# Two-layer sequence model on one core: a second unit's queries in other PSUM banks, a key head moved behind the first transposes, a norm's inverse root moved to another engine, and three output projections moved from places 101 and 111 to 73 and 81

## The chip, the cores and the metric

The kernel runs on one core of a Trainium2 chip. The metric is the device time of one execution in microseconds, of which three runs are given. The engines are named as the profile names them: PE multiplies matrices (PEld is its loading of weights), DVE is the vector engine, ACT the scalar engine, POOL the GpSimd engine, and SP issues most of the transfers. PSUM is the memory that PE writes its results to, in banks of 128 partitions by 512 numbers; the other engines read them there.

## The reference

2048 tokens (2 sequences of 1024) of 256 numbers pass two layers. Each layer is attention and then a feed-forward part, each with a residual sum and a norm behind it (x = layernorm(x + part(x))):

- layer 0: softmax attention with rotary positions (32 query heads, 8 key heads, causal), then a gated feed-forward part with 8-bit weights;
- layer 1: a gated delta rule with 16 heads of 128 by 128 state, then a feed-forward part whose weights are only signs.

The delta rule is where the change lies. Per head, q, k and v are projections of x, each passed through a causal convolution over 4 tokens and a silu; alpha and beta are sigmoids of two more projections; and then, token by token,

```
err = S k - v
S   = alpha * S - beta * err k^T
o   = S q
```

The rows o are normalised over 128 numbers per head, scaled by a sigmoid gate g = sigmoid(x Wg), and projected with Wo back to 256 numbers. Everything is float32.

## The kernel before, in words

**Stages.** Layer 0's attention comes first (two passes over the scores, L1267 and L1336), then its feed-forward part (up to about 800 us), then the delta rule (about 800 us to 1950 us), with the early parts of each stage laid into the stage before it, and layer 1's feed-forward part last. Products whose precision matters are made of three matmuls with high and low parts (`mm3`, L962 to L964).

**The delta rule's tiling.** The 2048 tokens are cut into 4 halves of 512, and the 16 heads into 8 pairs. A *unit* is one pair of heads in one half: unit i is half i // 8 and pair i % 8, so there are 32 units. Units 7, 15, 23 and 31 are the last ones of their halves. Inside a unit the tokens go through in 4 chunks of 128, the state M handed on from chunk to chunk (`recur`): transposed v minus the state's part (`pr`, L673 and L677), the copy `prs` on ACT, a product with the inverted triangle (`pw`, L688), the copy `wc` on ACT, the state's product (`pm`, L700) and the output's (`po`, L715 and L716), and the new state M on DVE (L705 or L707).

**The order.** Each unit has 120 *places*, 30 per chunk. Everything beside the recurrence is written as generators that yield the place at which they want to go on; `Places` runs them by that number, and this sets the written order of the program. `InLine` chains all of PE's matmuls in exactly this order from unit 0 on (`te.strict`). On the other engines a scheduler orders the instructions at build time; each engine's queue is then run in order.

In unit i, beside its own recurrence, the places hold work for later units: the next unit's v and q projections (`others`, places 1 and 31, through `pair`), its gate projection (61), its scores `pkq` (`scores`, L508, places 71 and 81), each followed by two products on POOL (`decayed`, L519 and L521) that scale k and q by decays `dg`; the keys of unit i + 4 (`keys`, place 91; the scans L325 on DVE); and for every other unit a solver on DVE (`blocks`, L384 and L390) and a set of small matmuls (`levels`, L420, then L423 on DVE, then L431).

Unit i's own rows are brought to an end in unit i + 1 by `finish`: a norm per head (inverse root on POOL through `rsqrt`, then L599 and the normalising instructions of DVE, ACT and POOL, L606 and L609), at places 41 and 51 the transposes `pt` (L615), then ACT (L618), the gate's product on DVE (L619), a rounded copy `yh` on POOL (L623) and the rest `yl` on POOL (L911); and at two more places the projection `pf` with Wo, 12 matmuls each for two chunks. DVE adds `pf` to the tokens `xtok` (L636). For the last unit of a half the tokens are then complete: a layernorm on DVE (L942, L943, L925 to L932, L946) and a store follow.

```
AT_FINISH, AT_FINISH_LAST, AT_HALF = (41, 51, 101, 111), (31, 41, 71, 76), ((22, 30, 46), (8, 13, 20))
```

The first two of each four are the places of `pt`, the other two those of `pf`.

**PSUM in the delta rule.** Tag `p` has 2 banks (projections and their convolutions), `m` has 2 (triangles, scores, keys' transposes), `c` has 2 (the recurrence), `t` has 1 (`pt` and `pf`), `l` has 1 (the levels).

**A projection's way.** `project` writes one head's product into a bank. `conv` reads it there on ACT and with two instructions on DVE (L275, the taps), `conv_out` reads it a last time on ACT (`far`, L289), and POOL adds `far` (L292). The bank is free after L289.

**The start.** Before the strict order begins, `rest_of_first` scales unit 0's k and q, projects unit 1's v and q and unit 4's k, in that order, all into the two `p` banks. At the same time layer 0's feed-forward part ends: its last block of 256 tokens is normalised (`layernorm`, with the inverse root on POOL, L934 to L937) and stored. `anchor["norm"]` is the last instruction of that norm (L946); the solver of unit 2 is ordered behind it.

Of the kernel before, what the change touches and what calls it, by code (L numbers as in the profile page):

```python
# [22 lines left out]
NT = B * T // P  # L23
# [8 lines left out]
HP = 2  # L32
NS = H // HP
# [44 lines left out]
AHEAD = 4  # L78
# [6 lines left out]
AT_ROWS, AT_QUERIES, AT_KC, AT_GATE, AT_GATE_ROWS, AT_SCORES = 1, 31, (42, 52), 61, 70.5, (71, 81)  # L85
AT_OUT = 9.5
# [2 lines left out]
AT_LEVELS = 43, 53, 73, 83, 103, 113, 132, 142  # L89
AT_FFN = 24  # L90
AT_FINISH, AT_FINISH_LAST, AT_HALF = (41, 51, 101, 111), (31, 41, 71, 76), ((22, 30, 46), (8, 13, 20))

FFN0, FFN1, FFN1_LAST, FFN1_TAIL = 7.6, 22.0, 27.0, 40.0

# [50 lines left out]
def delta_rule(  # L145
# [13 lines left out]
    nc = tc.nc  # L159
# [8 lines left out]
    ps_p = open_pool(left, "ps_p", "left", 2, PSUM)  # L168
    ps_m = open_pool(left, "ps_m", "left", 2, PSUM)
# [15 lines left out]
    def bank(pool, tag, name):  # L185
        return pool.tile([P, HT], F32, name=name, tag=tag)
# [49 lines left out]

        return divmod(i, NS)

    def project(m, i, h):
        hi, s = place(i)  # L240
        if h == 0 and ("w" + m) not in st[i]:
            st[i]["w" + m] = weights(m, s)
        wh, wl = st[i]["w" + m]
        xh, xl = halves[hi]["xh"], halves[hi]["xl"]
        pp = bank(ps_p, "p", "pp")
        hs = slice(h * P, (h + 1) * P)
        for k in range(2):
            mm3(pp, wh[:, k, hs], wl[:, k, hs], xh[:, k, :], xl[:, k, :], k == 0, k == 1)
        return pp
# [10 lines left out]
    def conv(m, i, h, pp):  # L260

        hi, s = place(i)
        n, hd = "qkv".index(m), s * HP + h
        acc = half_tile(early if m == "k" else conv_pool, m, 10 if m == "k" else 4)
        st[i][m, h] = acc

        with tc.high_priority():
            nc.scalar.activation(  # L268
                acc, pp, AF.Identity, bias=cb[:, n, hd : hd + 1], scale=cw[:, n, hd, KS - 1 : KS]
            )  # L270
            if hi % 2 == 0:
                nc.scalar.copy(halos[:, n, hd, :], pp[:, HT - KS + 1 :])  # L272

            for d in range(1, KS - 1):
                made = nc.vector.scalar_tensor_tensor(  # L275
                    acc[:, d:], pp[:, 0 : HT - d], cw[:, n, hd, KS - 1 - d : KS - d], acc[:, d:], ALU.mult, ALU.add
                )
                if m == "k" and d == 1 and solved:
                    after(made, solved[-1])
        return made  # L280
# [18 lines left out]
    def keys(i, t0):  # L299

        hi, s = place(i)
        col = halves[hi]["col"]
        pps = [project("k", i, h) for h in range(HP)]
        if i < last:
            st[i + 1]["wk"] = weights("k", place(i + 1)[1])
        for h in range(HP):
            taps = conv("k", i, h, pps[h])
        yield t0 + AT_OUT
        for h in range(HP):
            conv_out("k", i, h, pps[h])  # L310
        yield t0 + AT_DECAY - AT_KEYS
        lt = early.tile([P, U, P], F32, name="lt", tag="lt", bufs=4)
        st[i]["lt"] = lt
        nc.gpsimd.memset(lt[:, :, 0:1], 0.0)
        for h in range(HP):
            hd = s * HP + h
            dec = decay(hi, hd, 0, "da")
            d1 = early.tile([P, HC, P], F32, name="d1", tag="raw", bufs=RAW)
            nc.gpsimd.affine_select(
                d1, col[:, :, hd].unsqueeze(2).to_broadcast([P, HC, P]),  # L320
                pattern=[[0, HC], [1, P]], compare_op=ALU.is_equal, fill=0.0, base=0, channel_multiplier=-1,
            )
            e = half_tile(early, "at", 10)
            after(
                nc.vector.tensor_tensor_scan(e, dec, d1.rearrange("p c t -> p (c t)"), 0.0, ALU.mult, ALU.add), taps  # L325
            )
            st[i]["at", h] = e

            em = early.tile([P, HC], F32, name="em", tag="em", bufs=10)
            nc.gpsimd.tensor_scalar(em, q4(e)[:, :, P - 1], -SCALE, None, ALU.mult)  # L330
            st[i]["em", h] = em
        for h in range(HP):
            yield t0 + AT_TRIANGLE[h] - AT_KEYS
            e, k = st[i]["at", h], st[i]["k", h]
            pkk = bank(ps_m, "m", "pkk")
            for c in range(HC):
                t = slice(c * P, (c + 1) * P)
                te.link(nc.tensor.matmul(pkk[:, t], lhsT=k[:, t], rhs=k[:, t], start=True, stop=True))
            nc.vector.scalar_tensor_tensor(
                lt[:, h * HC : (h + 1) * HC, 1:P], q4(pkk)[:, :, 1:P], SCALE, q4(e)[:, :, 0 : P - 1],  # L340
                ALU.mult, ALU.mult,
            )
        yield t0 + AT_TRIANGLE[2] - AT_KEYS
        n = i % 2
        if n == 0:
            st[i]["d1"] = dram.tile([Q, 2 * U, BL, BL], F32, name="d1_", tag="d1_")
        else:
            st[i]["d1"] = st[i - 1]["d1"]
        for q in range(Q):
            r = slice(q * BL, (q + 1) * BL)  # L350
            nc.sync.dma_start(
                out=st[i]["d1"][q, n * U : (n + 1) * U].rearrange("u j t -> j u t"), in_=lt[r, :, r]
            )
# [124 lines left out]
                    te.link(nc.tensor.matmul(p4[A, u, :], lhsT=n3[Z, u, :], rhs=lt[Z, u, Z], start=True, stop=True))  # L478
            nc.scalar.copy(st[i + n]["lt"][A, :, Z], p4[A])

    def pair(m, i):

        pps = [project(m, i, h) for h in range(HP)]
        for h in range(HP):
            conv(m, i, h, pps[h])
        if i < last:
            yield AT_OUT
        for h in range(HP):
            conv_out(m, i, h, pps[h])
# [68 lines left out]
    def rest_of_first():  # L558
        decays(0)
        for which in "kq":  # L560
            for h in range(HP):
                decayed(0, h, which)
        te.strict, te.last = True, ended[0]
        for m in "vq":
            drain(pair(m, 1))
        ks = keys(AHEAD, AT_KEYS)
        next(ks)
        lines.add(ks, next(ks), 0)

    def gate_of_first():  # L570
        gate(0)
        yield GAP
        gate_rows(0)
# [70 lines left out]
    def recur(i):  # L644
# [8 lines left out]
        def moments(c):  # L653
            for h in range(HP):
                st6 = pools["late"].tile([P, 6], F32, name="ost", tag="ost")
                with tc.high_priority() if i == last and c == HC - 1 else nullcontext():
                    nc.vector.bn_stats(st6, o[:, c, h, :])
                    nc.vector.bn_aggr(m[:, c * HP + h, 0:2], st6)
            part = HC // 2 if i == last else HC
            if c % part == part - 1:  # L660
                chunks = range(c + 1 - part, c + 1)
                at = i * UNIT + 3 * GAP * (c + 1) + 3
                lines.add(finish(
                    i, o, m[:, chunks[0] * HP : (c + 1) * HP, :], chunks,
                    AT_HALF[c // part] if i == last else AT_FINISH_LAST if i == last - 1 else AT_FINISH,
                ), at, at if i == last else (i + 1) * UNIT)

        for c in range(HC):
# [166 lines left out]
    def drain(g):  # L835
        for _ in g:
            pass

    for i in range(-AHEAD, last + 1):
# [19 lines left out]
        elif 0 <= i < last:  # L859
            lines.add(others(i + 1), t + AT_ROWS, t)  # L860
        if i == 0:
            lines.add(gate_of_first(), t + AT_QUERIES)
        if i >= 0:
            lines.add(recur(i), t, chain=True)
# [27 lines left out]
def tile_two_layers(ctx: ExitStack, tc: tile.TileContext, a, out):  # L892
# [46 lines left out]
    def layernorm(pool, x, t0, n, tag="ln", eng=None):  # L939
        m = pool.tile([P, n, 11], F32, name=tag, tag=tag)  # L940
        for i in range(n):
            nc.vector.bn_stats(m[:, i, 5:11], x[:, t0 + i, :])  # L942
            nc.vector.bn_aggr(m[:, i, 0:2], m[:, i, 5:11])  # L943
        rsqrt(m[:, :, 2], m[:, :, 1], m[:, :, 3], m[:, :, 4], eng=eng)
        for i in range(n):
            made = nc.vector.tensor_scalar(  # L946
                x[:, t0 + i, :], x[:, t0 + i, :], m[:, i, 0:1], m[:, i, 2:3], ALU.subtract, ALU.mult
            )
        return made
# [16 lines left out]
    def after(later, earlier):  # L966

        tc.add_manual_dep(
            later.ins, earlier.ins.name,
            mybir.DependencyInfo(mybir.DependencyClass.NoSync, mybir.DependencyReason.DATA), reason="order",  # L970
        )
# [507 lines left out]
    def open_ffn(group):  # L1479
# [20 lines left out]
        def block(n):  # L1500
# [45 lines left out]
            with tc.high_priority() if n == NT - 2 else nullcontext():  # L1546
                for i in range(2):
                    y = new("fy", [P, E], 2)
                    nc.vector.tensor_mul(y, po[i], s_down)
                    nc.vector.tensor_add(x[:, n + i, :], y, x[:, n + i, :])  # L1550
                anchor["norm"] = layernorm(pool, x, n, 2, eng=nc.gpsimd)
                store_tokens(xs, n, x[:, n : n + 2, :])
            yield 0.2

# [127 lines left out]
```

## Time and profile before

| what | value |
|---|---|
| median of 3 runs | 2062.5 us (2060.35 to 2066.07) |
| the profiled execution's own time | 2059.24 us |
| its span | 2057.5 us |
| PE busy | 1894.6 us (92%) |
| DVE busy | 1469.6 us (71%) |
| ACT busy | 1271.6 us (62%) |
| POOL busy | 1078.6 us (52%) |
| mean granted PE clock | 0.977 |

How to read it: the span is what the profile covers; 1.74 us of the execution lie outside it. Busy shares are means over the whole span, so they hide single stretches. The rows of the window view give, for a stretch, each engine's busy time and the mean clock that PE was granted (1.00 is full speed). A row of the view of waits says which instruction of an engine stood idle for what, in total microseconds, times, and the longest. A row of the timeline gives start, duration, engine, line and operands; `x4` at its end means four instructions taken together, and what stands in brackets is the idle time before it and what ended it.

### The profile page before, as it was taken

What the parts mean: (1) busy time and instruction counts of PE and PEld (TensorE: products, weight loads), DVE (VectorE), ACT (ScalarE), POOL (GpSimd) and SP (SyncE); (2) the same over time, 40 slices, a digit from 0 to 9 for tenths busy, and PEclk for the clock granted to TensorE, in tenths of its full rate; (3) what the DMA queues carried; (4) which work ended last, traced back from release to release, by engine and by line L of the source; (5) the groups of instructions that cost most, each with busy time, mean ns of one, the idle gap of its engine ahead of it and who ended that gap; (6) DMA issues with size and microseconds to landing.
All of it is one profiled execution on the core that took longest, in us unless ns stands there. A gap on an engine that the chain in (4) does not pass through costs nothing. (4 is left out here: it accounts for less than half of the span.)

```text
span 2057.5 us, 49231 instructions
## 1 busy us (share of the span) xinstructions
PE 1894.6 (92%) x18657; PEld 1494.6 (73%) x18657; DVE 1469.6 (71%) x3469; ACT 1271.6 (62%) x2739; POOL 1078.6 (52%) x1739
## 2 busy tenths in 40 slices
PE   5898989999998998999999999998999999999886
PEld 3455555555555786889888888887988888888775
DVE  5756666877756986586778778678677778865565
ACT  1365556576664466667776776766677676676433
POOL 4353332431124565566776576666567666665452
PEclk9999999999999998999999999999999999999997
DMA  5563443441132432343444434344344434442010
GB/s 169 177 190 126 146 134 127 147 132 65 52 76 62 119 89 90 103 136 104 130 110 121 130 111 130 106 124 119 115 113 118 127 114 132 119 124 81 22 41 21
DMA packets 312998, 229.17 MB, mean 111 GB/s; under 512 B 139640, under 2 KB 278904, under 8 KB 312760
## 3 DMA queue, kind: packets, MB, share of 16 engines
q1 hardware_dynamic: 299640, 210.73, 35.1%
q10 hardware_dynamic: 9760, 10.83, 1.6%
q0 software_dynamic: 3360, 4.46, 0.9%
q8 instruction: 147, 2.41, 0.5%
q14 instruction: 91, 0.75, 0.1%
HBM read 171.18 MB, written 51.87 MB: 108 GB/s over the span
## 5 line engine op out<-in xcount | busy, mean ns | idle before, releaser
L1276 DVE TENSOR_REDUCE mx<-ps 128x4 f32<-128x1024 f32 (+1 forms) x320 | 344.1, 1111 | 129.3 <-PE ps L1267 86.8
L1340 ACT ACTIVATE es<-ps 128x512 f32<-128x512 f32 (+1 forms) x608 | 314.3, 578 | 128.7 <-PE ps L1336 117.1
L1336 PE MATMUL ps<-qT,kT 128*128 128x512 f32 (+3 forms) x768 | 220.7, 371 | 17.8 <-ACT es L1340 16.5
L1267 PE MATMUL ps<-kT,qT 128*128 128x512 f32 x576 | 198.7, 419 | 26.9 <-DVE mx L1276 17.6
L1336 PEld LDWEIGHTS ps<-qT,kT 128*128 128x128 f32 x768 | 130.9, 190 | 104.2 <-ACT es L1340 57.0
L1267 PEld LDWEIGHTS ps<-kT,qT 128*128 128x128 f32 x576 | 101.2, 190 | 86.8 <-DVE mx L1276 47.7
L289 ACT ACTIVATE far<-pp,cw 128x509 f32<-128x509 f32 x192 | 133.4, 700 | 46.3 <-DVE k L275 18.8
L1357 PE MATMUL av<-es,vaug 128*32 128x512 f32 (+3 forms) x1536 | 157.1, 495 | 0.7 <-POOL es L1343 0.7
L1343 POOL TENSOR_SCALAR_AFFINE_SELECT es<-es 128x512 f32<-128x512 f32 x128 | 80.5, 639 | 145.8 <-ACT es L1340 143.5
L911 POOL TENSOR_TENSOR wfl<-wf,wfh 128x256 fp32r<-128x256 f32 x80 | 58.7, 735 | 186.1 <-ACT wfh L1000 160.4
L275 DVE SCALAR_TENSOR_TENSOR q<-pp,cw,q 128x511 f32<-128x511 f32 (+1 forms) x128 | 93.2, 742 | 47.1 <-ACT halos L272 23.2
L275 DVE SCALAR_TENSOR_TENSOR k<-pp,cw,k 128x511 f32<-128x511 f32 (+1 forms) x128 | 92.2, 743 | 45.8 <-ACT k L268 25.1
L292 POOL TENSOR_TENSOR q<-q,far 128x509 f32<-128x509 f32 x64 | 69.4, 1087 | 95.3 <-ACT far L289 95.2
L275 DVE SCALAR_TENSOR_TENSOR v<-pp,cw,v 128x511 f32<-128x511 f32 (+1 forms) x128 | 92.2, 739 | 33.3 <-ACT v L268 18.2
L292 POOL TENSOR_TENSOR k<-k,far 128x509 f32<-128x509 f32 x64 | 77.8, 1217 | 51.2 <-ACT far L289 50.6
L519 POOL TENSOR_TENSOR k<-k,dg 128x508 f32<-128x508 f32 x64 | 82.2, 1284 | 33.7 <-PE pkq L508 29.4
L716 PE MATMUL po<-wc,at 128*128 128x128 f32 x512 | 97.3, 277 | 0.0
L680 ACT COPY prs<-pr 128x256 f32<-128x256 f32 x128 | 48.8, 382 | 76.5 <-PE pr L677 68.3
L1000 ACT CAST wfh<-wf 128x256 fp32r<-128x256 f32 x80 | 32.4, 405 | 102.5 <-DMA wf<-in_w1k 35.0
L325 DVE TENSOR_TENSOR_SCAN at<-da,d 128x512 f32<-128x512 f32 x64 | 90.4, 1453 | 0.0
L700 PE MATMUL pm<-wc,kc 128*128 128x128 f32 x448 | 77.7, 296 | 11.4 <-ACT wc L691 11.3
L715 PE MATMUL po<-M,q 128*128 128x128 f32 x448 | 87.8, 278 | 0.0
(325 smaller groups left out, 5907.8 us busy)
## 6 DMA issues: line engine op xcount, KB each, us to landing
wk<-w1k SPq DMA_DIRECT2D x64, 256.0 KB
da<-dec SPq DMA_DIRECT2D x64, 256.0 KB
wv<-w1v SPq DMA_DIRECT2D x64, 256.0 KB
wq<-w1q SPq DMA_DIRECT2D x64, 256.0 KB
dg<-dec SPq DMA_DIRECT2D x64, 256.0 KB
wg<-w1g SPq DMA_DIRECT2D x64, 256.0 KB
wo<-w1o SPq DMA_DIRECT2D x64, 256.0 KB
ad<-avs ACTq DMA_DIRECT2D x32, 256.0 KB
```

What stands on the lines that cost most here:

```text
L275: made = nc.vector.scalar_tensor_tensor(acc[:, d:], pp[:, 0 : HT - d], cw[:, n, hd, KS - 1 - d : KS - d], acc[:, d:], ALU.mult, ALU.add)
L289: made = nc.scalar.activation(far[:, w], pp[:, w], AF.Copy, scale=cw[:, n, hd, 0:1])
L292: nc.gpsimd.tensor_add(acc[:, KS - 1 :], acc[:, KS - 1 :], far[:, w])
L325: nc.vector.tensor_tensor_scan(e, dec, d1.rearrange("p c t -> p (c t)"), 0.0, ALU.mult, ALU.add), taps
L519: nc.gpsimd.tensor_mul(q4(k)[:, :, 1:P], q4(k)[:, :, 1:P], q4(gs)[:, :, 0 : P - 1])
L715: te.link(nc.tensor.matmul(po[:, r], lhsT=st[i]["q", h][:, t], rhs=M[:, r], start=True, stop=False))
L716: te.link(nc.tensor.matmul(po[:, r], lhsT=st[i]["at", h][:, t], rhs=wc[:, r], start=(M is None), stop=True))
L1267: anchor["mm"] = te.link(nc.tensor.matmul(ps[:, j - j0, :].rearrange("p (g k) -> p g k", k=P), lhsT=q_, rhs=kT[:, :, j * P : (j + 1) * P], ...
L1276: nc.vector.tensor_reduce(mx[:, it, j0 // 2, :], ps[:, 0:n, :].rearrange("p j (g k) -> p g j k", k=P), AX.XY, ALU.max)
L1336: te.link(nc.tensor.matmul(ps[:, g - g0, :], lhsT=kT[:, g, jb * P : (jb + 1) * P], rhs=qT[:, i0 : i0 + w], start=True, stop=True,))
L1340: exps.append(nc.scalar.activation(es[:, g0 : g0 + n, 0:w], ps, AF.Exp, scale=D ** -0.5))
L1357: mm = te.link(nc.tensor.matmul(av[ROW * g : ROW * (g + 1), i0 - ih * 512 : 512], lhsT=vaugs[b][:, jb, kv, :], rhs=es[:, g, 0:w], start=(j ...
```

## The change

1. `rest_of_first` projects unit 1's queries into the two `m` banks, while its values stay in the `p` banks. Unit 4's first key head is projected there too; the second key head and all that follows it goes into a stream of its own, `first_keys`, whose next place is after the first chunk has begun, so that the two first `pr` transposes of unit 0 stand ahead of it on PE. One of the taps of unit 1's queries is ordered behind `anchor["norm"]`.
2. The last block of layer 0's feed-forward part takes its norm's inverse root on DVE (three times L930 to L932) instead of POOL (three times L934 to L937).
3. Units 7, 15 and 23 (the last of a half, but for the very last) have their two `pf` groups at places 73 and 81 instead of 101 and 111, behind the scores of the next unit's heads.

```diff
+AT_FINISH_ROWS = 41, 51, 73, 81
...
-    def project(m, i, h):
+    def project(m, i, h, psum=None):
...
-        pp = bank(ps_p, "p", "pp")
+        pp = bank(*(psum or (ps_p, "p")), "pp")
...
+                if m == "q" and i == 1 and d == 1:
+                    after(made, anchor["norm"])
...
-        pps = [project("k", i, h) for h in range(HP)]
+        pps = [st[i].pop("first")] if "first" in st[i] else [project("k", i, 0)]
+        pps.append(project("k", i, 1))
...
-    def pair(m, i):
+    def pair(m, i, psum=None):
...
-        pps = [project(m, i, h) for h in range(HP)]
+        pps = [project(m, i, h, psum) for h in range(HP)]
...
-        for m in "vq":
-            drain(pair(m, 1))
+
+        for m, psum in (("v", (ps_p, "p")), ("q", (ps_m, "m"))):
+            drain(pair(m, 1, psum))
+        st[AHEAD]["first"] = project("k", AHEAD, 0)
+
+    def first_keys():
+
         ks = keys(AHEAD, AT_KEYS)
         next(ks)
-        lines.add(ks, next(ks), 0)
+        yield AT_ROWS + AT_OUT
+        yield next(ks)
+        yield from ks
...
-                    AT_HALF[c // part] if i == last else AT_FINISH_LAST if i == last - 1 else AT_FINISH,
+                    AT_HALF[c // part] if i == last else AT_FINISH_LAST if i == last - 1
+                    else AT_FINISH_ROWS if s == NS - 1 else AT_FINISH,
...
         if i == 0:
+            lines.add(first_keys(), t + AT_ROWS, t)
             lines.add(gate_of_first(), t + AT_QUERIES)
...
-                anchor["norm"] = layernorm(pool, x, n, 2, eng=nc.gpsimd)
+                anchor["norm"] = layernorm(pool, x, n, 2, eng=nc.gpsimd if n < NT - 2 else None)
```

## The prediction

> **What bounds the kernel now.** I read the page first, for which engine is the bound; then the stretches around the four places that the change touches, for clock and gaps; then PE's waits there; then POOL's timeline at the new place of the projections.
>
> ```profile
> PE 1894.6 (92%) x18657; PEld 1494.6 (73%) x18657; DVE 1469.6 (71%) x3469; ACT 1271.6 (62%) x2739; POOL 1078.6 (52%) x1739
> ```
>
> PE is busy for 92% of the span, so a microsecond taken from its idle time or from its half-speed time is a microsecond of the whole, unless the next wait takes it. The places touched are the start of the delta rule (seam 0, 800 us) and the ends of the first three halves (seams 1, 2 and 3: 1112, 1402 and 1702 us). The view by windows there (PE's busy time first, DVE's third, the granted clock after POOL):
>
> ```profile
> 800.00:820.00 20.00, 13.24 (x43) 8.99 (x42) 15.28 (x42) 11.09 (x24) 8.33 (x18) 0.76 0.41 131
> 820.00:840.00 20.00, 18.11 (x101) 15.85 (x102) 10.22 (x33) 8.76 (x24) 10.86 (x11) 0.77 0.64 185
> 1112.00:1146.00 34.00, 29.89 (x446) 26.66 (x445) 33.04 (x111) 21.00 (x46) 23.30 (x35) 1.00 0.42 121
> 1402.00:1428.00 26.00, 24.13 (x160) 21.16 (x159) 24.38 (x75) 15.44 (x37) 15.58 (x17) 1.00 0.46 133
> 1428.00:1444.00 16.00, 8.31 (x160) 7.03 (x159) 10.58 (x40) 7.19 (x16) 9.16 (x19) 0.68 0.34 107
> 1702.00:1730.00 28.00, 26.10 (x263) 22.96 (x263) 26.93 (x94) 16.09 (x33) 20.23 (x31) 1.00 0.47 132
> ```
>
> Seam 0 loses both ways: 6.8 us of gaps in its first window, and a clock of 0.76. At seams 1 to 3 DVE is nearly full (33.0 of 34 us), and PE loses a few microseconds after it. What PE waits for, seam by seam (total, times, longest):
>
> ```profile
> PE pp L962 <- ACT far L289: 5.9, 3, 2.1
> ```
>
> ```profile
> PE px L431 <- DVE n L423: 2.3, 1, 2.3
> PE pm L700 <- ACT wc L691: 1.4, 1, 1.4
> ```
>
> ```profile
> PE pt L615 <- POOL o L609: 7.7, 2, 7.1
> ```
>
> ```profile
> PE p L460 <- issue: 1.6, 1, 1.6
> PE pm L700 <- ACT wc L691: 1.4, 1, 1.4
> ```
>
> So there is 5.9 us to win at seam 0, and at most 3.7, 7.7 and 3.0 us at the others, if the earlier projections relieve DVE.
>
> **Part 1, seam 0: queries in the `m` banks, second key head later, inverse root on DVE.** The three waits for `far` (5.9 us) are for `p` banks. Queries no longer need them, key head 0 comes long after `far` of the values, and key head 1 moves behind the `pr` transposes. These three gaps go. What is late next: chunk 1 needs the state M from DVE (L705 at 824.0), which stands behind the two scans of unit 4's keys (819.83 to 823.9), and the change leaves scans ahead of it; by DVE's order M comes near 819.4, 4.6 us earlier. Then the gate's projection waits for `far` of key head 0, and chunk 1's `wc` copy on ACT stands behind the silu of the keys, which wait for POOL's adds; laid end to end the second `pm` comes at 828 to 829 instead of 831.08, a gain of 2 to 3 us. The inverse root: 12 POOL instructions between 806.63 and 810.87 go, 9 DVE instructions of about 0.15 us (1.35 us) come; the norm's end (813.0), the tokens' store and the `dg` loads queued behind it on SP come some 2 us sooner, and POOL's products, which now wait 2.61 us for `dg`, with them. No one on PE waits for these before chunk 1. Clock: rows here run at half speed from 812.1 to 829.2; fewer gaps may free it, but the waits that remain are of the size that halves it (below). Ends: −5.9 us (all gaps won) and 0 (the chain through M, keys and `wc` takes all). I take −1.5, by the `pm` row, less some for the 1.35 us on DVE and the new waits.
>
> **Part 2, seams 1 to 3: projections at 73 and 81.** The 24 matmuls of a seam cost the same wherever they stand (0.118 us apart, 1.43 us a group). What counts is what they wait for. The first group now stands directly behind `pkq` of head 0, and its sixth matmul reads `yl` of head 1 (L911). POOL's order is the same in both kernels, and there `yl` of head 1 stands *behind* the two products of head 0's decays (L519, L521), the first of which waits for just that `pkq`. Seam 3's timelines, POOL and then PE:
>
> ```profile
> 1703.73 0.61 POOL L623 CAST yh<-y 128x512 fp32r<-128x512 f32 x1 [0.90 <-DVE y L619]
> 1704.53 1.27 POOL L519 TENSOR_TENSOR k<-k,dg 128x508 f32<-128x508 f32 x1 [0.19 <-PE pkq L508]
> 1705.75 1.28 POOL L521 TENSOR_TENSOR q<-q,dg 128x512 f32<-128x512 f32 x1
> 1706.98 1.31 POOL L911 TENSOR_TENSOR yl<-y,yh 128x512 fp32r<-128x512 f32 x1
> ```
>
> ```profile
> 1703.39 1.06 PE L508 MATMUL pkq<-q,k 128*128 128x128 f32 x8
> 1704.29 0.61 PE L700 MATMUL pm<-wc,kc 128*128 128x128 f32 x4
> ```
>
> `pkq` ends at 1704.29 and `yl` at 1708.29: 4.0 us, of which five matmuls cover 0.6. So PE stands still for 3.4 us at each of three seams. Seams 1 and 2 have the same rows (`pkq` ends 1113.49 and 1405.55, `yl` ends 1117.48 and 1409.55). Queued behind the waiting matmul on PE: `pm`, `po`, the second `pkq`, and with them the new M, DVE's scores and POOL's second pair of products. This is certain as far as the orders are.
>
> The stall also costs clock. At 1743.98 PE idles for 1.64 us, and then 512-column matmuls come 0.43 us apart instead of 0.23 until 1750.8:
>
> ```profile
> 1747.40:1750.80 3.40, 3.40 (x10) 2.63 (x9) 0.44 (x1) 2.31 (x6) 0.00 (x0) 0.51 0.00 0
> 1750.80:1754.20 3.40, 3.40 (x34) 3.14 (x34) 2.65 (x6) 1.63 (x3) 1.06 (x2) 1.00 0.37 125
> ```
>
> 3.4 us at half speed lose 1.7 us of work; a 3.4 us stall may hit one or two such stretches, 1.6 to 3.0 us; I take 2.1. [...]
>
> A third term: in the last chunk the old group stood between `pw` and `po` while ACT made `wc`; without it PE waits for `wc`, about 0.7 us (the 0.46 and 1.4 us rows of `pm` from both sides). Each seam so begins at 3.4 + 2.1 + 0.7 = +6.2 us. What comes back, as DVE has its norm work (L636 to L946, some 9 us) earlier:
>
> - Seam 1: the 2.3 us before L431, because the four L946 no longer stand around L423: +3.9. The 1.4 us row could come back too: +2.5; nothing back: +6.2.
> - Seam 2: the normalise of unit 16 (L609) moves ahead of the queries' taps, and most of the norm stands in front of the scans; its last `pt` would end near 1436 instead of 1438.2, −2.2, and the half-speed stretch behind it (to 1443.4, 2.7 us lost) may shrink: −4.9. If DVE's key taps, late by the stall, hold the normalise: +1. I take −1.5.
> - Seam 3: 1.6 of the 3.0 us is "issue" before L460 (the levels), which the change does not touch; 1.4 comes back: +4.8, between +3 and +6.2.
>
> SP: one `dg` load, two `wk` loads move behind the solver's stores and the `wo` loads; `wk` is fetched a whole unit (36 us) ahead, and POOL reaches the second `dg` only behind `yl`: nothing, and at most the 2.61 us that the `dg` row at 818 shows. The second group waits for DVE to have added the first (same `t` bank); `pm`, `po` and `pkq` of 2.5 us lie between, against 0.68 for L636.
>
> **Sum.** −1.5 + 3.9 − 1.5 + 4.8 = +5.7 us on the profiled execution's 2059.24 (span 2057.5 and 1.74 around it), so 2064.9; that execution lies 3.3 us below the median of 2062.5, so 2068.2 beside it. What a measurement can tell from no change is about 0.3%, 6.2 us; the sum lies at that border.
>
> **Rivals.**
>
> 1. *The gaps are won, and clock with them* (faster). Place: seam 0 and seam 2. For it: 5.9 us of waits for banks plainly removed and 0.76 clock (17 us of half speed, some 6 to 8 us of work lost); the 7.1 us wait and its 2.7 us. Against it: the M and `wc` chain, and the stall. Price: −8 at seam 0, −4.9 at seam 2, +2.5 and +3 at the others: −7.4, 2055. It decides once seam 0's clock is back at full speed before 820.
> 2. *DVE becomes the bound behind the stall* (slower still). DVE is 33 of 34 us busy at seam 1; it idles through most of 3.4 us while PE waits, and the keys' taps and scans come late at all three seams. Price: nothing back at any seam, seam 0 zero: 3 × 6.2 = +18.6 at worst, with half of that +9 to +14: 2075.
> 3. *Stall and relief cancel*: the clock is not halved (−6.3 from the sum): 2062, within 0.3%.
> 4. *The stall doesn't occur* as POOL is early: excluded by its order, where L519 waits for `pkq`.
>
> **Numbers.** Forecast (the sum) 0.55, its own range 2062 to 2073, about evenly on both sides of the 0.3% border; rival 1: 0.19; rival 2: 0.17; rival 3: 0.09. Slower: 0.17 + 0.30 = 0.47; within: 0.25 + 0.08 = 0.33; faster: 0.20. The range from 2053 to 2077 leaves out the tails of rivals 1 and 2.
>
> **What would show it.** Waits `pf <- POOL yl` of about 3.4 us, three times, in the chain behind `pkq`, and clock under 1.00 near 1116, 1408 and 1708 would show the stall; the row `pp L962 <- ACT far` gone or near 2 us at 800, and M's copy near 819, seam 0; `px <- DVE n` gone at 1143, and `pt <- POOL o` under 3 us at 1430, the relief. It is wrong if no `yl` wait appears, or if seam 0 alone gives over 6 us.

## The result: 0.55% slower, within the range

The changed kernel takes 2069.69 us (median of 7 runs, 2065.99 to 2080.55), the kernel before, run again beside it, 2060.35 us (7 runs in all, 2055.25 to 2066.07). The ratio is 1.0055, with a 95% interval of 1.0035 to 1.0075: some 7 to 15 us lost. The forecast was 2068.2 us with a slight lean to slower, 1.5 us from the measured time. That it came so near is in part luck: it was the first median of the kernel before, 2062.5 us, plus 5.7 us, and that kernel came out 2.1 us lower when it was run again. What the change itself costs is 11 us by the ratio, about twice the 5.7 us of the sum.

The profiled execution of the changed kernel has a span of 2067.2 us, 9.7 us more than that of before (its own time is 2068.99 us, 9.75 us more). The page's first row shows that PE did the same work, and that DVE did the nine instructions more:

```profile
PE 1895.5 (92%) x18657; PEld 1495.1 (72%) x18657; DVE 1478.8 (72%) x3478; ACT 1270.6 (61%) x2739; POOL 1074.0 (52%) x1727
```

**One ruler for all kernels.** Line numbers and places shift from kernel to kernel, and so does the time at which the delta rule begins: the first value projection starts at 799.9 us in the kernel before, 799.6 in the changed one, and between 801.4 and 810.1 in the experiments, though no kernel alters anything ahead of it except what is named here. A span alone therefore can't carry a difference of a few microseconds. What can is a stretch with the same work in it. I use the starts of the `wc` copy of the first chunk of a unit, read from ACT's timeline: from unit 7 to unit 10 for seam 1, 15 to 18 for seam 2, 23 to 26 for seam 3. The view by windows of the kernel before over these three stretches (stretch, its length, then PE busy with its count; the clock stands after POOL):

```profile
1057.30:1171.04 113.74, 106.70 (x1536) 95.50 (x1537) 86.14 (x249) 76.50 (x165) 73.76 (x122) 1.00 0.44 127
1351.58:1469.96 118.38, 107.81 (x1525) 96.14 (x1526) 84.00 (x233) 78.46 (x184) 71.95 (x116) 0.96 0.42 123
1648.17:1762.37 114.20, 108.52 (x1536) 96.70 (x1537) 85.76 (x249) 76.17 (x165) 74.47 (x121) 0.99 0.42 125
```

and of the changed kernel over the same three:

```profile
1057.33:1175.69 118.36, 106.97 (x1536) 95.28 (x1537) 88.33 (x249) 76.72 (x166) 73.29 (x122) 1.00 0.42 123
1355.98:1472.66 116.68, 106.94 (x1525) 95.55 (x1526) 85.05 (x233) 77.56 (x185) 72.28 (x116) 0.99 0.44 126
1650.25:1770.67 120.42, 110.20 (x1536) 98.31 (x1537) 89.31 (x249) 76.89 (x165) 73.71 (x121) 0.97 0.40 117
```

The counts of PE agree row by row, so length minus busy is idle time, and the two larger differences in busy time at the same count go with the clock of the rows: 1.7 us more at seam 3, with 0.97 against 0.99, and 0.9 us less at seam 2, with 0.99 against 0.96. Seam 1: +4.6 us, nearly all idle (7.0 to 11.4). Seam 2: −1.7 (idle 10.6 to 9.7, busy −0.9). Seam 3: +6.2 (idle 5.7 to 10.2, busy +1.7). Together +9.1 of the 9.75 us; the start gives −0.4, and the rest of the span moves by +1.0. Each of these lengths comes from one profile. Stretches that no edit touches (units 2 to 7, 10 to 15 and 18 to 23, measured in the same way) differ by 0.9, 1.7 and 1.6 us among the twelve profiles of this document, so a difference under some 1.5 us in one stretch says little by itself. At the start the two windows shown before now read:

```profile
800.00:820.00 20.00, 14.13 (x54) 10.55 (x52) 18.67 (x50) 9.74 (x22) 6.54 (x5) 0.76 0.59 192
820.00:840.00 20.00, 16.71 (x94) 14.38 (x94) 8.58 (x37) 10.14 (x26) 10.96 (x13) 0.78 0.47 124
```

PE does more in the first and less in the second; the clock is as low as it was (0.76 and 0.78, before 0.76 and 0.77).

**The stall is there.** PE's waits at seam 3 in the changed kernel (total, times, longest):

```profile
PE pf L977 <- POOL yl L924: 3.3, 1, 3.3
PE pm L712 <- ACT wc L703: 1.6, 1, 1.6
PE pr L689 <- DVE M L719: 1.5, 1, 1.5
PE px L435 <- issue: 1.1, 1, 1.1
```

and the timelines there, POOL's first and then PE's (L523 and L525 are the decay products, L924 is `yl`, L512 the scores, L977 the matmul on `yl`):

```profile
1705.41 0.61 POOL L634 CAST yh<-y 128x512 fp32r<-128x512 f32 x1 [0.90 <-DVE y L630]
1706.21 1.27 POOL L523 TENSOR_TENSOR k<-k,dg 128x508 f32<-128x508 f32 x1 [0.20 <-PE pkq L512]
1707.45 1.26 POOL L525 TENSOR_TENSOR q<-q,dg 128x512 f32<-128x512 f32 x1
1708.67 1.26 POOL L924 TENSOR_TENSOR yl<-y,yh 128x512 fp32r<-128x512 f32 x1
```

```profile
1706.44 0.28 PE L976 MATMUL pf<-wo,yh 128*128 128x256 f32 x1
1709.98 0.58 PE L977 MATMUL pf<-wo,yl 128*128 128x256 f32 x1 [3.27 <-POOL yl L924]
```

`yh` is ready at 1706.02; POOL then does two products that PE does not wait for here, and only afterwards the `yl` that PE waits for. The same 3.3 us appear at seams 1 and 2: 9.8 us in three waits.

### The profile page after: what moved, and what is told of

It is laid out like the page before. It is cut to its first block, busy times and chain, and to the rows that moved or that the text cites. A ratio compares the mean times of both kernels' runs of the same rounds, so it can differ in the third digit from the quotient of the medians.

```text
span 2067.2 us, 49232 instructions
## 1 busy us (share of the span) xinstructions
PE 1895.5 (92%) x18657; PEld 1495.1 (72%) x18657; DVE 1478.8 (72%) x3478; ACT 1270.6 (61%) x2739; POOL 1074.0 (52%) x1727
## 5 line engine op out<-in xcount | busy, mean ns | idle before, releaser
L924 POOL TENSOR_TENSOR wfl<-wf,wfh 128x256 fp32r<-128x256 f32 x80 | 58.5, 734 | 185.0 <-ACT wfh L1013 153.6
L276 DVE SCALAR_TENSOR_TENSOR q<-pp,cw,q 128x510 f32<-128x510 f32 (+1 forms) x128 | 92.9, 743 | 46.1 <-ACT q L269 24.0
L523 POOL TENSOR_TENSOR k<-k,dg 128x508 f32<-128x508 f32 x64 | 81.7, 1276 | 56.7 <-PE pkq L512 47.0
L689 PE MATMUL pr<-M,k 128*128 128x128 f32 x448 | 83.4, 282 | 7.5 <-DVE M L719 3.9
L700 PEld LDWEIGHTS pw<-prs,lt 128*128 128x128 f32 x512 | 76.8, 191 | 18.3 <-ACT prs L692 7.6
```

The costliest lines, as they stand in the source:

```text
L276: made = nc.vector.scalar_tensor_tensor(acc[:, d:], pp[:, 0 : HT - d], cw[:, n, hd, KS - 1 - d : KS - d], acc[:, d:], ALU.mult, ALU.add)
L523: nc.gpsimd.tensor_mul(q4(k)[:, :, 1:P], q4(k)[:, :, 1:P], q4(gs)[:, :, 0 : P - 1])
L689: te.link(nc.tensor.matmul(pr[:, r], lhsT=st[i]["k", h][:, t], rhs=M[:, r], start=False, stop=True))
```

## The experiments

The lengths of the stretches, in microseconds, all from ACT's timelines in one profiled execution each; *start* is from the first value projection to unit 2's first `wc`. The ratio is that of the timed runs to the kernel before, with its 95% interval. The kernel before was run again beside each set: its median was 2060.35 us beside the changed kernel, 2063.7 beside e1 to e4, 2064.3 beside e5 to e8 and 2064.6 beside e9 and e10. So times of different sets are compared here by their ratios.

| kernel | start | seam 1 | seam 2 | seam 3 | ratio |
|---|---|---|---|---|---|
| before | 84.4 | 113.7 | 118.4 | 114.2 | |
| changed | 84.0 | 118.4 | 116.7 | 120.4 | 1.0055 (1.0035 to 1.0075) |
| e1: places 73 and 81 alone | 84.1 | 122.2 | 117.8 | 121.4 | 1.0085 (1.0057 to 1.0113) |
| e2: start alone | 83.9 | 111.0 | 118.0 | 111.0 | 0.9971 (0.9958 to 0.9985) |
| e3: changed, `yl` first | 82.9 | 116.8 | 112.5 | 117.0 | 1.0007 (0.9992 to 1.0023) |
| e4: changed, places 83 and 93 | 83.9 | 120.4 | 112.7 | 113.7 | 1.0002 (0.9986 to 1.0017) |
| e5: start, unit 15 at 83 and 93 | 83.5 | 110.6 | 112.9 | 112.2 | 0.9946 (0.9926 to 0.9966) |
| e6: as e3, norms left out | 83.3 | 113.6 | 110.9 | 111.7 | 0.9949 (0.9932 to 0.9967) |
| e7: as e2, norms left out | 83.8 | 110.8 | 108.7 | 109.9 | 0.9901 (0.9871 to 0.9931) |
| e8: as e2, root on POOL | 85.1 | 110.9 | 118.1 | 111.4 | 0.9999 (0.9985 to 1.0013) |
| e9: as e3, norms behind taps and M | 84.9 | 121.8 | 118.6 | 120.7 | 1.0071 (1.0053 to 1.0089) |
| e10: start, unit 15, `yl` first | 84.7 | 110.9 | 115.8 | 111.9 | 0.9969 (0.9953 to 0.9984) |

### The two halves of the change (e1 and e2)

e1 adds only the new places to the kernel before:

```diff
+AT_FINISH_ROWS = 41, 51, 73, 81
...
+                    else AT_FINISH_ROWS if s == NS - 1 else AT_FINISH,
```

> The kernel before with the places 73 and 81 alone. Theory (the stall of the first projection group on yl, which stands behind the scores' products on POOL, costs the time): three waits of pf on yl of 3.3 us; seam 1 about +5, seam 2 about -2, seam 3 about +6.5 us; whole 8 to 11 us over before. Rival (the start of the delta rule costs the time): not over 3 us.

e2 is the changed kernel without them:

```diff
-                    else AT_FINISH_ROWS if s == NS - 1 else AT_FINISH,
+                    else AT_FINISH,
```

> The change without the places 73 and 81: queries in the scores' banks, second key head later, inverse root on DVE. Theory: no wait on yl, start worth -3 to +1 us, whole 2055 to 2063. Rival (the start costs the time): 6 us or more over before.

Measured: the places alone cost 0.85% (17.5 us, more than the 8 to 11 expected), the start alone gains 0.29% (6 us). The product of the two ratios, 1.0056, is that of the whole change. So the loss is the places', and the rival that the start costs the time is out. The three waits on `yl` are there, 3.3 us each, as expected. The seam stretches of e1 differ from the kernel before by +8.4, −0.6 and +7.2 us, against +5, −2 and +6.5 expected; at seam 1, where the miss is largest, PE also waits 2.2 us for `far` and 1.5 us for M.

The gain of e2 is as expected in size, but it is not where the edit is. Its start is 0.5 us shorter, which is within the scatter; seams 1 and 3 are 2.7 and 3.2 us shorter, where e2 edits nothing. At seam 1, the scheduler, which orders the program as a whole, has put L423's counterpart ahead of more of the norm, and the wait for it falls from 2.3 us to the 0.8 of this row:

```profile
PE px L435 <- DVE n L427: 0.8, 1, 0.8
```

At seam 3, DVE's order is the same as before; what is gone is the 1.6 us gap marked "issue", of which 0.4 is left, and the half-clock stretch that followed it (the clock of the stretch is 1.00 against 0.99 before). All kernels here with the queries in the `m` banks, the norm and the old places at seam 3 (e2, e5, e8 and e10) have 111.0 to 112.2 us there, and the single profile of the kernel before has 114.2; why the gap is shorter in them, I can't say.

### The stall (e3 and e4)

e3 orders the two products of head 0 behind `yl` of head 1 at the three seams:

```diff
+            made = nc.gpsimd.tensor_mul(q4(k)[:, :, 1:P], q4(k)[:, :, 1:P], q4(gs)[:, :, 0 : P - 1])
+            if i > 1 and i % NS == 1 and h == 0:
+                after(made, anchor["yl"])
...
+            made = nc.gpsimd.tensor_mul(q, q, gs)
+            if i > 1 and i % NS == 1 and h == 0:
+                after(made, anchor["yl"])
...
+                anchor["yl"] = sub_low(nc.gpsimd if i < last else nc.vector, yl, y, yh)
```

> The change, with head 0's two decay products (POOL) of units 9, 17 and 25 ordered behind yl of head 1. Theory: the waits on yl fall from 3.3 to under 1.0 us each, no half-speed stretch follows them, and the whole falls by 7 to 15 us against the changed kernel, to 2054 to 2062. Rival (DVE is the bound there, the stall is only where the wait shows): the wait goes and waits on M, wc or far take its place; within 3 us of the changed kernel.

e4 leaves POOL alone and moves the projections on:

```diff
-AT_FINISH_ROWS = 41, 51, 73, 81
+AT_FINISH_ROWS = 41, 51, 83, 93
```

> The change, with places 83 and 93 instead of 73 and 81: the first group stands behind the second head's scores, the second behind the keys' projections. Theory: 2.3 us of PE's work now cover part of the 4.0 us until yl, so waits of about 1.2 us each, too short for half speed; 6 to 12 us under the changed kernel. Rival (DVE is the bound): within 3 us of it.

In e3 the three waits on `yl` sum to 1.8 us, the longest 0.7, no half-clock stretch is left in the three seams (all three rows have a clock of 1.00), and the kernel takes 2066.2 us, some 10 us less than the changed one by the two ratios:

```profile
1066.52:1183.35 116.83, 107.30 (x1536) 95.40 (x1537) 86.65 (x249) 76.70 (x165) 73.47 (x122) 1.00 0.43 124
1363.73:1476.23 112.50, 105.86 (x1525) 93.87 (x1526) 82.01 (x233) 77.89 (x184) 71.80 (x116) 1.00 0.45 129
1654.37:1771.32 116.95, 107.34 (x1536) 95.41 (x1537) 86.97 (x249) 77.08 (x166) 74.23 (x121) 1.00 0.44 122
```

The time of 2066.2 us itself lies above the 2054 to 2062 that was expected, because the kernel before ran 3.4 us slower in this set; the fall of some 10 us is inside the 7 to 15. So the stall was the largest single cost, as the theory has it. But that is not all. At seam 1, where no half clock followed the stall, the stretch fell by only 1.5 us of the 2.6 that the wait lost, and against e2 seams 1 and 3 are still 5.8 and 5.9 us too long, while seam 2 is 5.5 us shorter. PE's waits at seam 1 in e3 tell what is left:

```profile
PE pm L716 <- ACT wc L707: 2.6, 2, 1.7
PE pr L693 <- DVE M L723: 1.8, 1, 1.8
PE pp L979 <- ACT far L292: 1.4, 1, 1.4
PE pr L693 <- DVE M L721: 0.8, 1, 0.8
```

The second and third rows are new, they are the changed kernel's too (1.8 and 1.8 us there), and both lead to DVE. In the changed kernel's DVE timeline the keys' taps, whose first `pp` PE finishes at about 1123.8, begin at 1127.36, behind the norm of the finished rows; and M at 1139.76 stands behind the last step of that norm:

```profile
1126.64 0.73 DVE L959 TENSOR_SCALAR xtok<-xtok,ln 128x256 f32<-128x256 f32 x2
1127.36 0.74 DVE L276 SCALAR_TENSOR_TENSOR k<-pp,cw,k 128x511 f32<-128x511 f32 x1
...
1138.46 0.72 DVE L959 TENSOR_SCALAR xtok<-xtok,ln 128x256 f32<-128x256 f32 x2
1139.10 0.74 DVE L276 SCALAR_TENSOR_TENSOR v<-pp,cw,v 128x510 f32<-128x510 f32 x1
1139.76 0.59 DVE L719 SCALAR_TENSOR_TENSOR M<-M,ge,pm 128x128 f32<-128x128 f32 x2
```

e4's waits on `yl` are 1.0 to 1.1 us, as expected, and the whole is some 11 us under the changed kernel. That waits of this size are too short for half speed was my estimate. In the traces of the kernel before and of the changed kernel the clock is 1.00 around gaps of 1.10 us (before, up to 1280.55) and 1.20 us (changed, up to 1356.43). Seam 1 has no part in this: it takes 120.4 us, 2.1 more than in the changed kernel, with 4.7 us that PE now waits for the normalise.

### Is it DVE's norm? (e6 and e7)

Both leave out the layernorm of the rows of units 7, 15 and 23, so that the rows of the first three halves go on unnormalised; e6 does it in e3, and e7, the control, in e2:

```diff
-                if s == NS - 1:
+                if i == last:
                     layernorm(gx, x, c1 + c0, 2, eng=nc.gpsimd if i == last and not final else None)
```

> The kernel with yl first, its layernorms of the first three halves left out (the rows stay unnormalised). Theory now: without the stall, seams 1 and 3 are still 6 us longer than with the start alone because DVE's norm work stands in front of M and of the keys' taps; without the norm they come within 2 us of the same kernel with the places 101 and 111. Rival (what is lost is the projections' cover for the wc copy, or POOL's later decays): still 4 us or more longer.

> The control to the run before: the start of the change alone, places 101 and 111, with the layernorms of the first three halves left out. Seam 2 loses most of its 7.1 us wait; seams 1 and 3 fall by 1 to 3 us.

With the norm the early places cost 5.8 and 5.9 us at seams 1 and 3 (e3 less e2); without it 2.8 and 1.8 (e6 less e7). So about half of what e3 left at seam 1, and some 70% at seam 3, is DVE's norm, as far as one profile of each kernel can tell. Seam 2 of e7 lost 9.3 us against e2, and PE's wait for the normalise there fell from 7.7 to 1.0; its seams 1 and 3 fell by 0.2 and 1.1 us against e2, less than the 1 to 3 us expected at seam 1, and by 2.9 and 4.3 against the kernel before. The rest, at seam 1 somewhat more than the 2 us I allowed, goes at least in part to small waits from the projections' own place, seen in e6's waits at seam 1:

```profile
PE pf L981 <- POOL yl L928: 0.7, 1, 0.7
PE pt L630 <- POOL o L624: 0.7, 1, 0.7
PE pf L979 <- DVE xtok L651: 0.5, 1, 0.5
PE po L732 <- ACT wc L707: 0.5, 1, 0.5
```

The last row is the lost cover of the `wc` copy. The norm itself is some 5 to 6 us of DVE at a seam: without it DVE's busy time at seam 1 falls by 5.1 us in the new places (86.65 in e3's first row, 81.56 in e6) and by 6.0 in the old ones (85.79 in e2, 79.76 in e7). In the old places its cost in time is small at seams 1 and 3 (0.2 and 1.1 us) and large at seam 2 (9.3 us).

### Where else the norm could stand (e9)

e9 is e3 with the norm alone written at places 101 and 111, and its first instructions ordered behind the keys' taps and M:

```diff
+        if s == NS - 1 and i < last:
+            for c0 in range(0, nc_, 2):
+                yield AT_FINISH[2 + c0 // 2]
+                layernorm(gx, x, c1 + c0, 2, behind=(anchor["taps"], updated[-1]))
```

> The kernel with yl first and projections at 73 and 81, but with the norm of the finished rows written at places 101 and 111 again and ordered behind the keys' taps and M on DVE. Theory (at seams 1 and 3 the norm in front of M and of the keys' taps costs what is left): there the waits of PE on M behind the norm (1.8 us) and on far before the values (1.2 to 1.4 us) fall under 0.5 us each, and the stretches fall by 2 to 4 us against the kernel with yl first; at seam 2 the wait for the normalise returns and the stretch is 4 to 6 us longer. Rival: the two waits stay, and the stretches are the same within 1 us.

The two waits are gone, as the theory said: at seams 1 and 3 no wait on `far` and only the 0.8 us on M that the kernel before has too. The stretches did not fall, though. They grew by 5.0 and 3.7 us, because the wait for the normalise, which I had expected at seam 2 alone (there the stretch grew by 6.1 us), is now at every seam (6.8, 6.9 and 6.8 us); the mean granted clock of e9's executions is 0.971 to 0.975, that of e3's 0.975 to 0.980. The first rows of PE's waits at seam 1:

```profile
PE pt L630 <- POOL o L624: 6.8, 2, 6.2
PE pm L721 <- ACT wc L712: 1.7, 1, 1.7
```

DVE's timeline there has the norm's last four instructions directly ahead of its part of the normalise (L624):

```profile
1147.32 2.27 DVE L970 TENSOR_SCALAR xtok<-xtok,ln 128x256 f32<-128x256 f32 x4
1149.51 0.16 DVE L614 SCALAR_TENSOR_TENSOR om<-om 128x8 f32<-128x8 f32 x1
1149.59 0.59 DVE L624 TENSOR_SCALAR o<-o,om 128x128 f32<-128x128 f32 x2
```

So the norm delays whatever DVE does next, and the price depends on what that is: the taps and M (some 3 us of waits at a seam in e3), or the normalise of the next unit's rows (over 6 us at a seam in e9, and the lower mean clock).

### One seam alone (e5 and e10)

If the seams are separate, early projections pay at seam 2 only. e5 is the start of the change with unit 15 alone moved, to where e4 had it; e10 moves it to 73 and 81 with `yl` first:

```diff
-                    else AT_FINISH_ROWS if s == NS - 1 else AT_FINISH,
+                    else AT_FINISH_ROWS if i == 2 * NS - 1 else AT_FINISH,
```

> The start of the change (queries in the scores' banks, second key head later, root on DVE) with early projections at one seam alone: unit 15 at places 83 and 93. If seams are separate and seam 2 is the one where DVE's earlier norm work relieves the normalise (7.1 us before), the stretch from unit 15 to 18 falls by 5 to 6 us against before, seams 1 and 3 stay as with the start alone, and the whole is 2046 to 2056, faster than both kernels. If the gain at seam 2 is made up by later waits: 2058 to 2062.

> The start of the change with early projections at unit 15 alone, at places 73 and 81 with yl first. Theory: seam 2 falls by 5.5 to 6 us against before as with yl first at all seams, seams 1 and 3 stay as with the start alone; 2046 to 2056, within 3 us of the kernel with unit 15 at 83 and 93. Rival (the seams' gains don't add): over 2058.

e5 takes 2050.3 us, ratio 0.9946 (0.9926 to 0.9966): faster than both kernels. Its seam 2 is 5.5 us shorter than before, and the 7.7 us wait for the normalise, still whole in e2, is no longer among its waits. The first three of them there:

```profile
PE pm L712 <- ACT wc L703: 2.5, 3, 1.2
PE pr L689 <- DVE M L717: 2.0, 1, 2.0
PE pf L977 <- POOL yl L924: 1.0, 1, 1.0
```

e10 won only 2.6 of its 5.5 to 6 us at seam 2, since PE waits for M there for 4.3 us in two waits. Its 2058.2 us miss the theory's 2046 to 2056 and just reach the rival's figure, and by the ratios it is 4.7 us slower than e5, not within 3. The rival's reason does not hold, though: seams 1 and 3 stay as in e2 (110.9 and 111.9 us), and it is seam 2 itself that gained less. The same edge on POOL that gave e3 112.5 us at this seam gave e10 115.8: one edge elsewhere, and the scheduler orders DVE differently.

### The start (e8)

e8 is e2 with the last block's inverse root back on POOL:

```diff
-                anchor["norm"] = layernorm(pool, x, n, 2, eng=nc.gpsimd if n < NT - 2 else None)
+                anchor["norm"] = layernorm(pool, x, n, 2, eng=nc.gpsimd)
```

> The start of the change with the last block's inverse root back on POOL. If the first prs copy waits for the memory of the normalised rows, which are stored only behind the norm, it comes about 2 us later than the 813.1 of the changed kernel (counted from the first value projection), and the first chunk with it; the rest of the start absorbs it, and the whole stays within 3 us of the start alone. Rival (the prs copy waits for the keys' taps on DVE): it comes earlier, as DVE has less to do.

The start is 1.1 us longer than e2's. The first `prs` copy comes 13.65 us after the first value projection, against 12.60 to 12.65 in e2 to e6, which have the root on DVE; the other four with the root on DVE have 13.45 to 13.74. The changed kernel, with 13.47, is one of these: its first value matmuls are 0.43 us apart up to 801.32 us and then 0.23. Counted from ACT's last read of unit 4's second key head before it (the copy into `halos`), which comes after those matmuls, the copy starts 3.00 us later in e2 and in the changed kernel, and 3.99 in e8. It comes later although DVE has less to do, so it does not wait for the taps. In e8, ACT's timeline names the store of the normalised rows:

```profile
816.30 0.37 ACT L692 COPY prs<-pr 128x256 f32<-128x256 f32 x1 [3.84 <-DMA xs<-x]
```

In the changed kernel that store is issued at 809.64 us, the load that reads it back at 812.99, and `prs` starts at 813.09, which fits the same cause. The view names a tap of the keys on DVE there, as it does in e2; that tap ends within 0.04 us of the copy's start. I take it to be the store in these too, since in e8 the copy came later although DVE had less to do. The copy came 1.0 us later in e8 than in e2, not 2: the store was issued 2.15 us later, but the copy started 2.3 us after the issue instead of 3.5. As to the whole, e8 is 5.8 us slower than e2 by the two ratios, more than the 3 us I allowed. Where that lies the profiles can't show: their stretches differ by 1.1 us at the start and 0.1 to 0.4 at the seams, and the profiled execution of e8 (2055.6 us) was faster than that of e2 (2062.0).

## Why the prediction held, and where it did not

**The stall: right.** 3.4 us at each of three seams, from the order on POOL; measured 3.26 to 3.27. (The prediction took the start of the next matmul, 1704.29, for the end of `pkq`; the row itself ends at 1704.45.) e3, which removes only its cause, gave back about 10 us.

**The clock: right mechanism, uneven size.** The forecast had 2.1 us at each seam. In the changed kernel, the view by windows behind the three stalls shows full clock at seam 1, 3.4 us at half clock at seam 2, and 6.7 at seam 3:

```profile
1113.60:1122.00 8.40, 5.14 (x45) 5.08 (x45) 7.27 (x27) 1.23 (x3) 4.93 (x5) 1.00 0.32 83
1416.00:1419.40 3.40, 3.40 (x19) 3.40 (x19) 2.70 (x13) 0.37 (x1) 0.00 (x0) 0.53 0.27 55
1709.50:1716.20 6.70, 6.21 (x29) 6.22 (x30) 4.55 (x24) 0.74 (x2) 0.43 (x2) 0.50 0.29 71
```

That is 0, 1.7 and 3.4 us of work lost, 5.1 against 6.3 forecast. At seam 2 the half-clock stretch of the kernel before, which ended at 1443.5, is gone, and at seam 3 so is its stretch of 3.4 us; the forecast had counted on neither in full. (The gap of 1.64 us that the prediction puts at 1743.98 runs from 1744.38 to 1746.02; the half clock behind it begins at 1747.32.)

**The lost cover of `wc`: right.** 0.7 us forecast; measured 0.5 us on `po` and 0.2 more on `pm` (1.6 against 1.4).

**"What comes back, as DVE has its norm work earlier": this step failed at seams 1 and 3.** The 2.3 us before L431 did come back. But the step counted only waits that end, and took DVE's norm as work out of the way; in its new place it stands in front of the keys' taps and of M. The changed kernel waits 1.8 us on M and 1.8 us on `far` at seam 1 and 1.5 us on M at seam 3, none of which was in the sum; e3, e6 and e7 show that these are the norm's (in e6 only 0.4 us on this M is left, at seam 3). At seam 1 they outweigh the clock that wasn't lost, so that +3.9 was measured as +4.6. At seam 3 the 1.5 us on M come on top, and the 1.4 us of `pm` on `wc`, which the forecast took back, stayed (1.6 in the changed kernel); with the half-clock stretch and part of the "issue" gap of before gone, +4.8 became +6.2. Seam 2, forecast at −1.5, was −1.7, but the figure was a choice between −4.9 and +1 and its agreement is in part luck: PE's wait of 7.7 us for the normalise went whole, and the stall of 3.3 us and other new waits (2.6 us on `pr` for ACT's copy of `o` among them) took most of it back. In the rivals the mechanism had its place, as DVE becoming the bound behind the stall; the runs show it as a part of the case and not as one instead of it.

**The start: the gaps went, as said, and so did most of the gain.** −1.5 us forecast, −0.4 measured, which is within the scatter: the kernels with this start lie between 82.9 and 84.9 us, e1 with the old one at 84.1. The three waits for `p` banks are gone (of the engines beside PE, only ACT and DVE read PE's results in the traces of the kernel before and of the changed one; none of POOL's 1739 and 1727 instructions does): PE runs from the first value projection to 809.4 us without a gap, and M is made at 818.4 instead of 824.0. The second `pm`, forecast for 828 to 829, starts at 829.95, against 831.08 before. What took the place of the three gaps was in part as forecast (2.2 us on `far` before the gate's projection, and the same 17 us at half clock, 811.65 to 828.72), and in part was not foreseen: `prs` waits, for the store as I take it, and PE for `prs`:

```profile
PE pw L700 <- ACT prs L692: 4.1, 1, 4.1
PE pp L975 <- ACT far L292: 2.2, 1, 2.2
```

e2 shows, with 0.9971, a gain of the start's edits that the forecast had nowhere: it comes through the scheduler's new order at seam 1, and at seam 3 through a gap that I can't explain. In the changed kernel the costs of the new places outweigh both.

**The rivals.** That the gaps and the clock of the start decide it is out: the start's clock is not back at full speed before 820. That the clock isn't halved holds for one seam in three. That the stall does not occur was excluded, rightly.

## What to carry to other kernels

When an operation is moved ahead on one engine, look up on every other engine what feeds it, and where that stands in the queue: a consumer placed ahead of its producer's turn waits for work that has nothing to do with it (3.3 us at each of three seams here). Then ask what the earlier result sets going: the norm's 5 to 6 us had to be done somewhere on a nearly full DVE (33.0 of 34 us at seam 1 before), and where it went had a large part in whether a seam gained 5.1 us (seam 2 in e5) or lost 6 (seams 1 and 3 in e3), both against e2. An edit that helps at one of three like places need not help at the others, so try each alone, and compare stretches with equal work rather than spans.

## What the runs showed of the hardware

The same stall of 3.3 us was followed by 0, 3.4 and 6.8 us at half clock at the three seams of the changed kernel. At seam 2 the half clock began 1.3 us after the stall's end (1415.81 against 1414.48 us), at seam 3 0.6 us before it (1709.36 against 1709.98). In the traces of the two kernels the half-clock stretches of the delta rule are 3.41, 6.83, 10.24 and 17.07 us long. The length of a gap alone did not tell whether one followed: after 1.64 us without work, up to 1746.02 in the kernel before, PE had 3.4 us at half clock; after 2.26 us, up to 1144.30 in the same kernel, it had none (clock 1.00 from 1144.3 to 1154.3); and after 3.26 us, up to 1116.92 at seam 1 of the changed kernel, it had none either (1.00 from 1113.6 to 1122.0). What decides it, no run here shows.
